# Turning the first expert tile's rows behind column tile 25 instead of 29 of the last attention block, in a graph attention and mixture-of-experts kernel

## The chip, the cores and the metric

The kernel runs on one core of a Trainium2 chip. A core has five engines that each work through a queue of their own: TensorE (PE, matmuls; its weight loads are listed as PEld), VectorE (DVE), ScalarE (ACT), GpSimd (POOL) and SyncE (SP, which here only issues DMAs). They wait for each other by semaphores. Matmul results go to PSUM, all other tiles lie in SBUF, and 16 DMA engines move data between these and HBM.

The metric is the time of one execution on the device in microseconds, as the median of several runs.

## The reference

One layer on 4096 tokens of width 256: a graph attention with four heads of 64 over a dense 4096 x 4096 adjacency, then a mixture of eight experts of which each token takes two. Both have a residual and a layer norm ahead.

```python
h = jnp.einsum('nd,hdk->hnk', x, W)
s_col = jnp.einsum('hnk,hk->hn', h, a1)
s_row = jnp.einsum('hnk,hk->hn', h, a2)
e = jax.nn.leaky_relu(s_row[:, :, None] + s_col[:, None, :], negative_slope=0.2)
e = jnp.where(adj[None, :, :] > 0, e, NEG_INF)
att = jax.nn.softmax(e, axis=-1)
h_prime = jnp.einsum('hij,hjk->hik', att, h)
out = jnp.transpose(h_prime, (1, 0, 2)).reshape(N, OUT_DIM)
y = jax.nn.elu(out) + x @ Wr + br
attention = gamma * (y - mean(y)) / sqrt(var(y) + LN_EPS) + beta
...
top_w, top_i = jax.lax.top_k(xf @ Wg + bg, 2)
top_w = jax.nn.softmax(top_w, axis=-1)
for e in range(8):
    h = jax.nn.gelu(xf @ W1[e] + b1[e], approximate=False)   # 256 -> 1024
    out = out + w_dense[:, e:e + 1] * (h @ W2[e] + b2[e])    # 1024 -> 256
```

## The kernel before

**Attention.** The 4096 rows are worked through in four blocks `a` of 1024 rows, and in each block the 4096 columns in 32 column tiles `j` of 128. A column tile has three steps. ScalarE turns the tile of the adjacency into a mask `am` (L1606). VectorE makes the unnormalised weights `w` of the four heads, one instruction of 128 x 1024 per head (L1689); ten buffers for `w` let it run up to two and a half tiles ahead of TensorE. TensorE then adds the weighted rows of each head into `acc` (L1198) and the sums of the weights into `den` (L1207). A matmul of `acc` fills 32 columns of the array and one of `den` two, and both are placed in different column groups, so that several run side by side. All of TensorE's instructions here hang on one hand-written chain: `queue` gives each an order behind the one queued last, and `order_of` does this for the small products in between, as long as `strict` is set.

**Between the tiles.** When a block is done, `finish_blocks(a)` works off what is left for its rows (normalising, elu, residual, both layer norms, the router's choice) in small steps: it is a generator, and one step is taken behind each column tile of the following block. Its last step is taken about tile 25; it works out each row's places in the experts' lists and issues 16 indirect DMAs on GpSimd (L1385), which scatter the rows, with their weights and ids, into `lists` in HBM. In this text, that is the scatter.

**The first expert tile.** In the last block, `a + 1 == NR`, the start of the expert stage is prepared within the attention. Behind tile 3, `plan_early` chooses the first expert tiles from what the lists hold so far, and `first_tile` asks for the first one's 256 rows, `xr0` (`load_rows_of`, issued at L571), and its first weights, `w10` (L600). Behind tile 29, `turn_first` turns those rows: `turn_rows_of` makes four transposes of 128 x 128 on TensorE (L607) into two PSUM banks `pt`, and copies each bank to `xT0` (L609). With `strict` set both copies are ScalarE's. Then `gelu_next` runs one activation on one column of `xT0` (L1589), whose only use is that the gelu table is loaded into ScalarE ahead of the first real gelu.

**After the last tile.** ScalarE and VectorE read `acc` and `den` (L1513, L1516, L1519). The pools of the attention are closed, and the expert stage's own tiles take their memory, so its loads can be issued only then. The loop over the expert tiles has two products each: `up` (L1872, with a gelu at L1876) and `down` (L1906). The rest of the last 1024 rows (`last_block`) goes in between them.

Of the kernel before, what the change touches and what calls it, by code (L numbers as in the profile page):

```python
# [44 lines left out]
def gat_then_moe(  # L45
# [23 lines left out]
    NT = N // P  # L69
# [6 lines left out]
    NR = N // R  # L76
# [142 lines left out]
    def forward(apart, stack):  # L219
# [39 lines left out]
        def turn_biases():  # L259
            pb = bank([P, E * FC], "pb")  # L260
            order_of(nc.tensor.transpose(pb, b1r, ident[: E * FC, : E * FC]))
            nc.vector.tensor_copy(bT, pb.rearrange("p (e f) -> p f e", e=E))
# [340 lines left out]
        def turn_rows_of(xr, xT):  # L603
            for c in range(DC):
                pt = bank([P, TT], "pt")
                for k in range(TT // CH):
                    order_of(nc.tensor.transpose(pt[:, ts(k, CH)], xr[:, k, ts(c, P)], ident))  # L607
                if c % 2 == 0 or strict[0] or (ordered[0] and given_out):
                    nc.scalar.copy(xT[:, c, :], pt)  # L609
                else:  # L610
                    nc.vector.tensor_copy(xT[:, c, :], pt)
# [3 lines left out]
        with ExitStack() as layer:  # L615
# [89 lines left out]
            def bounds_checked():  # L705

                nc.vector.tensor_reduce(strayed, limit, AX.X, OP.max)
                nc.vector.tensor_scalar(strayed, strayed, 0.5 * SPREAD, None, op0=OP.is_gt)
# [106 lines left out]
            def in_trace_order(start):  # L815

                before = {}
                for ins in nc.cur_bb.bb.instructions[start:]:
                    if ins.engine in before:
                        tc.add_manual_dep(  # L820
                            ins, before[ins.engine],
                            mybir.DependencyInfo(
                                mybir.DependencyClass.NoSync, mybir.DependencyReason.DATA
                            ),
                            reason="the order of the opening",
                        )
                    before[ins.engine] = ins.name
# [205 lines left out]
            def norm_steps(b):  # L1033

                with tc.issue_after(marks["top"]):
                    found = measured(b, fetched.pop(b))
                yield
                for t in range(TB):
                    normal_row(found, t)
                yield  # L1040
                pt = banks_turned()
                for t in range(TB):
                    turn_row(pt, found[0], t)
                keep_turned(b, pt)
                if b + 1 < NB:
                    fetched[b + 1] = rows_loaded(b + 1)
# [28 lines left out]
            def numbers_made():  # L1075

                if not apart:
                    nc.vector.tensor_scalar(brm, brm, -1.0, None, op0=OP.add)
                made_of_numbers()
# [132 lines left out]
            def attend(w, j, halves, sums_first=None):  # L1212


                def first_heads():
                    for half in halves:
                        for h in (1, 0):
                            rows_of_head(w, j, half, h)

                def other_heads():  # L1220
                    for half in halves:
                        for h in (1, 0):
                            weights_of_head(w, j, half, h)
                        rows_of_head(w, j, half, 2)
                    for half in halves:
                        rows_of_head(w, j, half, 3)
                        for h in (3, 2):
                            weights_of_head(w, j, half, h)

                parts = (first_heads, other_heads)  # L1230
                if sums_first is None:
                    sums_first = j in (0, NT - 1)
                for add in reversed(parts) if sums_first else parts:
                    add()
# [350 lines left out]
            def turn_first():  # L1585
                turn_rows_of(xr0, xT0)

            def gelu_next(known):
                nc.scalar.activation(warm, known, AF.Gelu)  # L1589
# [89 lines left out]
            else:  # L1679

                with tc.tile_pool(name="sep", bufs=2) as work:

                    def weigh(er, am, j, halves):
                        these = slice(halves[0], halves[-1] + 1)
                        mask = am.rearrange("p (s r) -> p s r", s=HB)
                        w = [[None] * H for half in range(HB)]
                        for h in ORDER:
                            wh = work.tile([P, HB, B], F32, tag="w", name="w", bufs=10)
                            marks["w"] = nc.vector.scalar_tensor_tensor(  # L1689
                                wh[:, these], er[:, these, h], eb[:, j, h : h + 1], mask[:, these],  # L1690
                                op0=OP.max, op1=OP.min,
                            ).ins
                            for half in range(HB):
                                w[half][h] = wh[:, half]
                        return w

                    both = list(range(HB))
                    ers = [er0, er1]
                    er = er0
                    pending = None  # L1700
                    norms, steps_of = {}, {}
                    ordered[0] = strict[0] = True
                    opened = len(nc.cur_bb.bb.instructions)
                    row = first_phase(weigh, norms)
                    in_trace_order(opened)
                    ordered[0] = False
                    with tc.issue_after(marks["w"]):
                        numbers_made()
                        bounds_checked()

                    def prepare_at(s):

                        for b in range(2, NB):
                            first = TB * b
                            if first - 3 <= s < first:
                                if b not in norms:
                                    norms[b] = norm_steps(b)
                                next(norms[b], None)
                            if first <= s < first + 4:
                                if s == first:  # L1720
                                    steps_of[b] = project_steps(b, True)
                                next(steps_of[b], None)

                    for j in range(TB):
                        prepare_at(TB + j)
                        attend(weigh(er, first_masks[:, j], j, [1]), j, [1])
                        if j == 0:
                            sums_turned(row)
                    for a in range(NR):
                        later = None  # L1730
                        for j in range(0 if a else TB, NT):
                            attend(
                                weigh(er, load_mask(a, j), j, both), j, both,
                                False if (a, j) == (NR - 1, NT - 1) else None,
                            )
                            if a == 0:
                                prepare_at(TB + j)
                            if pending:
                                next(pending, None)
                            if a == 1 and j == 1:  # L1740
                                turn_biases()
                            if a + 1 == NR and j == 3:
                                with tc.issue_after(marks["w"]):
                                    plan_early()
                                first_tile()
                            if a + 1 == NR and j == 29:
                                turn_first()
                                gelu_next(xT0[:, DC - 1, :1])
                            if j == 20 and a + 1 < NR:
                                later = ers[(a + 1) % 2]  # L1750
                                load_rows(later, (a + 1) * HB, HB, nc.scalar)
                        if a == 0:
                            mean_of_h()
                        er = later
                        if a + 1 < NR:
                            pending = finish_blocks(a)
                            next(pending)
                    strict[0] = False
# [350 lines left out]
```

## Time and profile before

| what | us |
|---|---|
| median of three runs | 1261.13 |
| lowest and highest of them | 1259.64, 1261.76 |
| the profiled execution's own time | 1260.56 |
| its span, first instruction to last | 1258.8 |
| last attention block ends, first expert matmul starts | 781.88 |
| PE, DVE, ACT, POOL busy | 1241.7, 845.5, 448.3, 240.4 |

The span is what the profile's shares refer to; all times in the text count from its start. A line of a timeline gives the start, the length, the engine, the line of the kernel, the operation, the tiles out<-in with their sizes, how many instructions are merged, and in brackets the engine's idle time before it with what ended that. "issue" means that the profile shows no wait, "remote" that a semaphore rose without an instruction that the profile could name. The start of a matmul is recorded, its end is modelled. A line of the table of stretches gives the stretch, its length, and then the busy time of PE, PEld, DVE, ACT and POOL with the number of their instructions, the clock granted to TensorE and the share of the DMA engines in use.

### The profile page before, as it was taken

To read this page: it belongs to the slowest core of one execution; us is meant where nothing else is said; L and a number is where in the kernel's file an instruction comes from. 1 tells how busy PE (TensorE), PEld (TensorE's weight loads), DVE (VectorE), ACT (ScalarE), POOL (GpSimd) and SP (SyncE) were. 2 spreads that over 40 slices of the span, in tenths; PEclk is the share of its full clock that TensorE was granted. 3 is DMA by queue.
4 is the path that set the end of the run, shared out by engine and by line. 5 is a ranking of instruction groups with operands and counts; after the bars stand their busy time and mean duration, and the time that the engine had idled before them with its cause. 6 is when DMAs were issued, how large, how long until landed. Compare 5 with 4: busy or idle time off the path is not lost.

```text
span 1258.8 us, 22720 instructions
## 1 busy us (share of the span) xinstructions
PE 1241.7 (99%) x8872; PEld 650.4 (52%) x8872; DVE 845.5 (67%) x1566; ACT 448.3 (36%) x918; POOL 240.4 (19%) x217
## 2 busy tenths in 40 slices
PE   9999999999999999999999999999999999999997
PEld 5444444332233332333325324888888876666686
DVE  7998887879999999999999995855111111111120
ACT  4332322265522365322655221533332332222322
POOL 4000000001002601006110024125322222122222
PEclk9999999999999999999999999999999999999999
DMA  6334433536533646334375422868998895455662
GB/s 215 118 118 126 155 107 102 166 104 145 177 114 103 225 112 201 116 94 158 107 178 183 133 70 77 276 171 219 259 236 239 227 219 116 102 139 105 140 160 37
DMA packets 155541, 190.23 MB, mean 151 GB/s; under 512 B 72312, under 2 KB 125680, under 8 KB 155040
## 3 DMA queue, kind: packets, MB, share of 16 engines
q1 hardware_dynamic: 133392, 145.39, 39.7%
q0 software_dynamic: 20544, 36.74, 13.2%
q10 hardware_dynamic: 1488, 6.55, 1.4%
q8 instruction: 71, 1.16, 0.4%
q14 instruction: 46, 0.38, 0.1%
HBM read 155.77 MB, written 29.74 MB: 147 GB/s over the span
## 4 chain that ended last, share of the span: by engine, by line
PE 93%; DVE 3%; issue 1%; ACT 1%; DMA 1%; POOLq 0%; SPq 0%; DVEq 0%; ACTq 0%
PE acc L1198 33%; PE po L1906 18%; PE ph L1872 17%; PE den L1207 17%; PE pr L1053 2%; DVE w L1689 2%; PE ph L1101 2%; PE ptx L1253 0%; DMA early<-lists 0%; PE acc L894 0%; PE pt L780 0%; PE ptr L1491 0%; PE po L1945 0%; PE pl L1264 0%; PE po L875 0%
## 5 line engine op out<-in xcount | busy, mean ns | idle before, releaser
L1198 PE MATMUL acc<-w,ha 128*32 128x512 f32 x4096 | 672.1, 593 | 2.3 <-ACT u L1401 0.9
L1689 DVE SCALAR_TENSOR_TENSOR w<-er,eb,am 128x1024 f32<-128x1024 f32 x496 | 605.9, 1275 | 36.2 <-PE den L1207 30.3
L1207 PE MATMUL den<-w,unit 128*2 128x512 f32 x2048 | 469.2, 592 | 0.4 <-issue 0.3
L1198 PEld LDWEIGHTS acc<-w,ha 128*32 128x32 f32 x4096 | 186.7, 110 | 293.7 <-issue 254.3
L1606 ACT ACTIVATE am<-adj 128x1024 bf16<-128x1024 int32 x124 | 130.6, 1054 | 347.8 <-DVE w L1689 213.1
L1872 PE MATMUL ph<-xT,w 128*128 128x256 f32 (+5 forms) x864 | 230.2, 424 | 2.1 <-issue 1.9
L1906 PE MATMUL po<-w,hT 128*128 128x256 f32 (+1 forms) x1040 | 229.7, 379 | 0.0
L1876 ACT ACTIVATE hT<-ph,bias 128x256 f32<-128x256 f32 (+5 forms) x216 | 111.1, 517 | 290.2 <-issue 185.8
L1906 PEld LDWEIGHTS po<-w,hT 128*128 128x128 f32 (+1 forms) x1040 | 195.7, 189 | 31.2 <-issue 3.1
L1919 DVE SCALAR_TENSOR_TENSOR o<-po,share,b2s 128x256 f32<-128x256 f32 (+2 forms) x66 | 31.7, 482 | 250.2 <-PE po L1906 211.4
L1872 PEld LDWEIGHTS ph<-xT,w 128*128 128x128 f32 x864 | 163.4, 190 | 62.0 <-issue 40.3
L1207 PEld LDWEIGHTS den<-w,unit 128*2 128x2 f32 x2048 | 94.7, 85 | 148.5 <-issue 140.0
L1931 POOL DMA_INDIRECT out<-o,ids x66 | 102.0, 1546 | 321.9 <-DMA out<-o,ids 136.4
L1385 POOL DMA_INDIRECT lists<-xe,at x64 | 88.3, 1379 | 267.6 <-issue 184.7
L1856 DVE STREAM_TRANSPOSE xT<-xr 128x512 f32<-128x512 f32 (+5 forms) x21 | 17.8, 850 | 34.0 <-PE ph L1872 31.2
L1053 PE MATMUL pr<-wr,xT 128*128 128x256 f32 x128 | 30.4, 381 | 0.2 <-ACT er L1147 0.2
L1894 ACT ACTIVATE b2s<-b2b,share 128x256 f32<-128x256 f32 x68 | 30.1, 499 | 0.0
L1121 POOL DMA_DIRECT2D residual<-rb x6 | 4.7, 784 | 121.2 <-DVE rb L1068 121.2
L1441 POOL DMA_DIRECT2D xf<-in_x x6 | 8.1, 1351 | 102.2 <-ACT xf L1440 102.2
L1053 PEld LDWEIGHTS pr<-wr,xT 128*128 128x128 f32 x128 | 24.1, 190 | 5.4 <-issue 0.9
L1101 PE MATMUL ph<-wall,xT 128*128 128x264 f32 x96 | 24.6, 399 | 0.0
L207 ACT ACTIVATE m<-y,off 128x256 f32<-128x256 f32 x48 | 23.7, 495 | 1.1 <-DVE off L215 0.6
(394 smaller groups left out, 618.8 us busy)
## 6 DMA issues: line engine op xcount, KB each, us to landing
adj<-in_adj SPq DMA_DIRECT2D x126, 512.0 KB
w<-in_L_ffn_W SPq DMA_DIRECT2D x54, 1024.0 KB
er<-parts ACTq DMA_DIRECT2D x3, 2048.0 KB
lists<-zeros POOLq DMA_DIRECT2D x8, 520.0 KB
residual<-rb POOLq DMA_DIRECT2D x8, 512.0 KB
rb<-residual SPq DMA_DIRECT2D x8, 512.0 KB
out<-y POOLq DMA_DIRECT2D x8, 512.0 KB
xb<-in_x SPq DMA_DIRECT2D x7, 512.0 KB
```

Of the source, the lines that this page charges most:

```text
L1053: order_of(nc.tensor.matmul(pr[:, k, :], turned[b][:, c, ts(t0 + k, P)], wr[:, c, :], start=(c == 0), stop=(c == DC - 1),))
L1101: order_of(nc.tensor.matmul(phs[t - t0], xT[:, c, ts(t, P)], wall[:, c, :], start=(c == 0), stop=(c == DC - 1),))
L1198: queue(nc.tensor.matmul(acc[half][h // 2][here : here + Q, :], ha[:, j, h * K + g * Q : h * K + (g + 1) * Q], w[half][h], start=(j == 0), ...
L1207: queue(nc.tensor.matmul(den[here : here + HB, :], unit[:, j, h, 1 - half : 1 - half + HB], w[half][h], start=(j == 0 and half == 0), stop ...
L1385: ins = nc.gpsimd.indirect_dma_start(lists, bass.IndirectOffsetOnAxis(ap=at[:, k, t : t + 1], axis=0), xe[:, t, :], None,).ins
L1606: nc.scalar.activation(am, at, AF.Relu, scale=2.0)
L1689: marks["w"] = nc.vector.scalar_tensor_tensor(wh[:, these], er[:, these, h], eb[:, j, h : h + 1], mask[:, these], op0=OP.max, op1=OP.min,).ins
L1872: order_of(nc.tensor.matmul(ph, job["w1"][:, c, ts(f, P)], xT[:, c, :], start=(c == 0), stop=(c == DC - 1),))
L1876: job["gelu"] = nc.scalar.activation(hT[:, f, :], ph, AF.Gelu, bias=job["bias"][:, f : f + 1]).ins
L1906: order_of(nc.tensor.matmul(po[:size], hT[:, f, k * CH : k * CH + size], w2[:, f, :], start=(f == 0), stop=(f == FC - 1),))
L1919: given_out.append(nc.vector.scalar_tensor_tensor(o[:size], po[:size], share[:size, k : k + 1], b2s[k][:size], op0=OP.mult, op1=OP.add,).ins)
L1931: added.append(add().ins)
```

## The change

`turn_first` is called behind column tile 25 of the last block, four tiles earlier. `gelu_next` stands alone behind the last column tile, 31, two tiles later than before. Nothing else is edited: the same instructions are issued, on the same engines and with the same buffers.

```diff
                                 with tc.issue_after(marks["w"]):
                                     plan_early()
                                 first_tile()
-                            if a + 1 == NR and j == 29:
+                            if a + 1 == NR and j == 25:
                                 turn_first()
+                            if a + 1 == NR and j == NT - 1:
                                 gelu_next(xT0[:, DC - 1, :1])
                             if j == 20 and a + 1 < NR:
                                 later = ers[(a + 1) % 2]
```

The two functions that it calls, and the one below them:

```python
def turn_first():
    turn_rows_of(xr0, xT0)

def gelu_next(known):
    nc.scalar.activation(warm, known, AF.Gelu)

def turn_rows_of(xr, xT):
    for c in range(DC):
        pt = bank([P, TT], "pt")
        for k in range(TT // CH):
            order_of(nc.tensor.transpose(pt[:, ts(k, CH)], xr[:, k, ts(c, P)], ident))
        if c % 2 == 0 or strict[0] or (ordered[0] and given_out):
            nc.scalar.copy(xT[:, c, :], pt)
        else:
            nc.vector.tensor_copy(xT[:, c, :], pt)
```

## The prediction

> **What bounds the kernel now.** I read the page first, then the chain of waits around the end of the last attention block, then the timeline of each engine there, then the times of single column tiles.
>
> ```profile
> span 1258.8 us, 22720 instructions
> ...
> PE 1241.7 (99%) x8872; PEld 650.4 (52%) x8872; DVE 845.5 (67%) x1566; ACT 448.3 (36%) x918; POOL 240.4 (19%) x217
> ...
> PE 93%; DVE 3%; issue 1%; ACT 1%; DMA 1%; POOLq 0%; SPq 0%; DVEq 0%; ACTq 0%
> ```
>
> TensorE carries 93% of the chain, so a microsecond of TensorE in the attention block or after it is a microsecond of the kernel, and an edit on ScalarE counts only if TensorE ends up waiting for it. But busy TensorE isn't TensorE at its rate, so I looked at the timeline of TensorE where the turn stands:
>
> ```profile
> 755.68 1.90 PE L1198 MATMUL acc<-w,ha 128*32 128x512 f32 x16
> ...
> 760.83 1.90 PE L1198 MATMUL acc<-w,ha 128*32 128x512 f32 x16
> ...
> 766.45 1.02 PE L1207 MATMUL den<-w,unit 128*2 128x512 f32 x2 [0.28 <-issue]
> 767.40 0.83 PE L607 MATMUL pt<-ident,xr 128*128 128x128 f32 x4
> 768.15 2.49 PE L1198 MATMUL acc<-w,ha 128*32 128x512 f32 x6
> 771.47 1.46 PE L1198 MATMUL acc<-w,ha 128*32 128x512 f32 x7 [0.82 <-issue]
> ```
>
> A column tile begins with the sixteen acc matmuls. Tiles 28 and 29 begin 5.15 us apart (755.68, 760.83), as nearly all do. Then tile 29 lasts to 768.15 with the turn (L607) at its end: 7.32 us. Tile 30's sixteen matmuls, 1.90 us elsewhere, come as six, an idle gap, seven and three more. The stretches of TensorE from tile start to tile start show the loss:
>
> ```profile
> 755.68:760.83 5.15, 5.15 (x52) 1.51 (x48) 4.89 (x5) 0.00 (x0) 4.23 (x4) 1.00 0.27 96
> 760.83:768.15 7.32, 7.04 (x56) 2.06 (x48) 3.46 (x3) 0.00 (x0) 5.49 (x7) 1.00 0.29 99
> 768.15:776.08 7.93, 6.98 (x47) 2.85 (x50) 2.57 (x2) 2.13 (x4) 1.91 (x2) 1.00 0.14 50
> 592.52:597.69 5.17, 5.17 (x54) 1.62 (x50) 5.17 (x5) 1.06 (x1) 4.33 (x3) 1.00 0.46 130
> ```
>
> The columns are length, busy time of PE, PEld, DVE, ACT and POOL with counts, granted clock and DMA share. The clock is 1.00 throughout, and the last line is a tile under the same scatter of rows (POOL L1385) one block earlier: no loss. Who waits meanwhile, on VectorE, ScalarE and GpSimd:
>
> ```profile
> 769.37 1.28 DVE L1689 SCALAR_TENSOR_TENSOR w<-er,eb,am 128x1024 f32<-128x1024 f32 x1 [5.09 <-PE pt L607]
> 771.49 1.28 DVE L1689 SCALAR_TENSOR_TENSOR w<-er,eb,am 128x1024 f32<-128x1024 f32 x1 [0.83 <-remote]
> ```
> ```profile
> 751.95 1.06 ACT L1606 ACTIVATE am<-adj 128x1024 bf16<-128x1024 int32 x1 [3.72 <-DVE w L1689]
> 772.37 0.65 ACT L609 COPY xT<-pt 128x256 f32<-128x256 f32 x2 [19.37 <-remote]
> 773.04 1.28 ACT L1589 ACT_TABLE_LOAD   x1
> ...
> 777.69 0.69 ACT L1513 ACTIVATE u<-acc,hbar 128x512 f32<-128x512 f32 x1 [3.16 <-PE acc L1198]
> ```
> ```profile
> 745.49 1.29 POOL L1385 DMA_INDIRECT lists<-xe,at  x1 [81.93 <-DVE at L1345]
> ...
> 769.39 0.97 POOL L1385 DMA_INDIRECT lists<-xe,at  x1 [0.30 <-issue]
> ```
>
> The transposes are recorded at 767.40 to 768.23, yet their copies on ScalarE start at 772.37, and the w that waits for tile 29's den (issued at 763.84) starts at 769.37. TensorE's word that it is done comes 4 to 5 us late, TensorE itself creeps, and all of it ends as the scatter (sixteen indirect DMAs, 745.49 to 769.39) ends.
>
> [...] Identity at 777.69 follows the gelu load without another.
>
> **The change part by part.**
>
> 1. The turn, moved from behind tile 29 to behind tile 25. It is four transposes of 0.27 to 0.33 us on TensorE and two copies of 0.38 us on ScalarE; it issues no DMA and passes no work of SP's or POOL's queue (the rows were asked for at 632.0 and must only have landed). Its price on TensorE: eight transposes (ptx, L1253) stretch a tile from 5.15 to 6.32 us (701.15 to 707.47), so 0.146 us each, 0.58 for four. It is paid before and after: 0.
>
> 2. The stall around it. Tile 29: 7.32 - 5.15 - 0.58 = 1.59 us. Tile 30: 7.93 - 5.15 = 2.78 us. Together 4.37 us. Is it the turn's, or the scatter's? The first sign of slowness on TensorE is the last den of tile 29 (a pair elsewhere, one by one here, 765.14 to 766.88), right at the turn; and the scatters of the two blocks before (399 to 433, 572 to 601) cost no column tile anything. Bounds: nothing gained if the scatter stalls whatever stands there, all 4.37 if it takes both. Behind tile 25 TensorE is at 745.38, just ahead of the first indirect DMA. I take 4.37 gained.
>
> 3. ScalarE's queue. The copies now come at about 746.2, between the masks am at 741.45 and 747.16. At worst they stand ahead of the earlier of these and hold it until 747, 5.5 us later than now; its first reader is the w at 751.78, so some 4 us of cover are left. Cost 0. Uncovered it would be 5.5 us of VectorE, which has ten w buffers (2.5 tiles, 12.9 us) of lead besides.
>
> 4. The w behind it. TensorE gives its 0.58 us at tile 25, so VectorE's buffers come free that much later: covered by the same lead. If the stall goes, the last two w (needed in tile 31) start at about 765 and 766 instead of 769.37 and 771.49.
>
> 5. The gelu table, moved to behind tile 31. One load of 1.28 us and one activation of 0.20 us. ScalarE has nothing from 753.0 (end of the last mask) to the first accumulator read at 777.69, apart from the copies. The load waits for no matmul of tile 31, only for the copies, so it may run right behind the mask. If it came behind the reads instead, ScalarE is idle from 779.24 to 782.00 and covers 1.48 us. The first gelu (783.80) waits for VectorE's bias. Cost 0; with cover gone 1.48 us.
>
> 6. What is late next. When attention ends 4.37 us sooner, the first expert tile needs xT0 and w10 (both asked for by 633.1). All other loads (SP from 782.16) are issued when the attention's memory is free and move along; the last scatter's landing at about 771.7 is still earlier than the end of attention at about 777.5. So the gain goes through to the end.
>
> Sum: 0 - 4.37 + 0. The profiled execution took 1260.56 us (span 1258.8 and 1.76 around it) and should take 1256.2, span 1254.4. The median of the runs is 0.57 above the profiled one: 1261.13 - 4.37 = 1256.8 us.
>
> **The rivals.**
>
> A, no change: the scatter's tail stalls TensorE and its semaphores whatever it is doing. For it: the den at 763.84 is already answered late, before the turn is reached; ten indirect DMAs follow at 1.27 us each there, faster than in the blocks before (mostly 2.3). Against it: the two clean scatters. Time 1261.1, within 1259.7 to 1262.0.
>
> B, part of it: only the part behind the turn (tile 30's 2.78) goes and the rest stays as the scatter's. 1258.3. It belongs to the faster cases.
>
> C, slower: transposes under a running scatter are what stalls TensorE, and behind tile 25 all sixteen indirect DMAs are still to come instead of two or three. The stall then happens at about 746, at the same price of 4.4 us, and what the scatter's end does to tile 29 stays: 1261.1 + 4.4 = 1265.5. It decides from the point where the new stall exceeds what leaves tile 29 and 30 by 2.5 us. For it: ptx transposes were never under a scatter in attention. Against it: at 745.38 the first indirect DMA isn't yet issued, and the turn takes under 1 us.
>
> **How the numbers follow.** Forecast with B: 0.57 (B 0.12 of it). A: 0.27. C: 0.16. About 0.2%, 2.5 us, is what a measurement of this kernel can tell from no change. The likeliest case alone runs from 1255.6 (4.37 and all of the 0.58, plus the spread of runs) to 1258.6. With A the range reaches to 1262.0, leaving C out: 1255.6 to 1262.0. Faster 0.57, same 0.27, slower 0.16.
>
> **What would show it.** In the new trace: L607 at about 745.4, its copies within 1 us of it, tile 25 with the turn at 5.75 us, tiles 29 and 30 at 5.15 each, the w no longer idle for 5 us, first expert matmul at about 777.5 instead of 781.88. A is right if tiles 29 and 30 still lose over 3 us without the turn; C if tile 25 or 26 loses over 2 us. I am wrong on ScalarE if a mask runs late and VectorE waits for it, or if the gelu load is found between the last matmul and the first gelu.

## The result, and the profile after

In 22 runs of each kernel, the changed one took 1258.28 us (1254.23 to 1263.21) and the kernel before 1261.57 (1259.33 to 1269.50). The chip of this comparison has no number on record and is called the first here. The ratio is 0.997, with a 95% interval of 0.9959 to 0.9981: 3.3 us shorter, between 2.4 and 5.2. The profiled execution took 1258.36 us, 2.2 less than that of before. The forecast was 1256.8 in a range of 1255.6 to 1262.0.

The page after, with the same three lines as before:

```profile
span 1256.7 us, 22720 instructions
...
PE 1239.8 (99%) x8872; PEld 647.8 (52%) x8872; DVE 845.1 (67%) x1566; ACT 448.2 (36%) x918; POOL 241.3 (19%) x217
...
PE 93%; DVE 3%; issue 1%; ACT 1%; DMA 1%; another core or an unknown queue 0%; POOLq 0%; SPq 0%; DVEq 0%; ACTq 0%
```

TensorE's busy time fell by 1.9 us: part of its stall was listed as busy. The stretches after, for tile 25 with the turn and for tiles 29 and 30:

```profile
740.24:746.11 5.87, 5.87 (x56) 1.82 (x53) 5.80 (x10) 1.06 (x1) 0.59 (x1) 1.00 0.09 38
761.58:766.73 5.15, 5.15 (x52) 1.51 (x48) 4.88 (x5) 0.00 (x0) 4.24 (x4) 1.00 0.24 82
766.73:771.88 5.15, 5.15 (x52) 1.51 (x48) 0.97 (x1) 0.00 (x0) 3.52 (x4) 1.00 0.26 91
```

Tiles 29 and 30 take 10.30 us instead of 15.25, and tile 25 pays 0.72 us for the turn. Who waited, on ScalarE and VectorE, after:

```profile
747.19 1.06 ACT L1606 ACTIVATE am<-adj 128x1024 bf16<-128x1024 int32 x1 [4.66 <-DVE w L1689]
748.15 0.63 ACT L609 COPY xT<-pt 128x256 f32<-128x256 f32 x2
748.80 1.28 ACT L1589 ACT_TABLE_LOAD   x1
...
752.29 1.06 ACT L1606 ACTIVATE am<-adj 128x1024 bf16<-128x1024 int32 x1 [1.99 <-DVE w L1689]
772.99 0.69 ACT L1513 ACTIVATE u<-acc,hbar 128x512 f32<-128x512 f32 x1 [19.65 <-PE acc L1198]
```
```profile
760.07 4.88 DVE L1689 SCALAR_TENSOR_TENSOR w<-er,eb,am 128x1024 f32<-128x1024 f32 x4 [0.27 <-PE den L1207]
765.22 2.48 DVE L1689 SCALAR_TENSOR_TENSOR w<-er,eb,am 128x1024 f32<-128x1024 f32 x2 [0.27 <-PE den L1207]
```

The 5.09 us of VectorE before its second last `w` are 0.27 now. The copies of the turn stand behind a mask and wait for nothing further, and the gelu table's load has slipped in ahead of the last mask, which it doesn't delay: that mask still waits 1.99 us for VectorE. The first expert matmul (L1873, one line lower than before) starts at 777.15 instead of 781.88, 4.73 us sooner. Yet the span shrank by only 2.1. The rest is lost a hundred microseconds later, beside the second scatter of the last rows (L1385, 868.92 to 878.84); TensorE's and ScalarE's timelines after:

```profile
871.74 5.34 PE L1873 MATMUL ph<-xT,w 128*128 128x256 f32 x24
877.40 1.13 PE L1873 MATMUL ph<-xT,w 128*128 128x256 f32 x4 [0.32 <-issue]
880.98 2.08 PE L1873 MATMUL ph<-xT,w 128*128 128x256 f32 x4 [2.45 <-ACT hT L1877]
```
```profile
876.87 0.47 ACT L1877 ACTIVATE hT<-ph,bias 128x256 f32<-128x256 f32 x1 [1.87 <-PE ph L1873]
880.46 1.20 ACT L1877 ACTIVATE hT<-ph,bias 128x256 f32<-128x256 f32 x3 [3.11 <-remote]
```

The product `up` has 32 matmuls; 28 are out by 878.5, ScalarE's gelus of them are released only at 880.46, and TensorE waits 2.45 us for these. Then the stretches show a thing that was not there before, a granted clock of 0.57:

```profile
880.00:884.00 4.00, 3.02 (x7) 2.48 (x8) 0.00 (x0) 2.11 (x6) 1.07 (x2) 0.57 0.48 109
```

The clock's record has half speed from 880.5 to 883.9. Compared instruction by instruction in TensorE's order, the changed kernel is 4.69 us ahead of the kernel before at 870 us, and 2.11 us ahead from 890 us to the end.

### The profile page after: what moved, and what is told of

The parts are those of the page before. It is cut to its first block, busy times and chain, and to the rows that moved or that the text cites. A ratio compares the mean times of both kernels' runs of the same rounds, so it can differ in the third digit from the quotient of the medians.

```text
span 1256.7 us, 22720 instructions
## 1 busy us (share of the span) xinstructions
PE 1239.8 (99%) x8872; PEld 647.8 (52%) x8872; DVE 845.1 (67%) x1566; ACT 448.2 (36%) x918; POOL 241.3 (19%) x217
## 2 busy tenths in 40 slices
DMA packets 155541, 190.23 MB, mean 151 GB/s; under 512 B 72312, under 2 KB 125680, under 8 KB 155040
## 4 chain that ended last, share of the span: by engine, by line
PE 93%; DVE 3%; issue 1%; ACT 1%; DMA 1%; another core or an unknown queue 0%; POOLq 0%; SPq 0%; DVEq 0%; ACTq 0%
PE acc L1198 33%; PE po L1907 18%; PE ph L1873 17%; PE den L1207 17%; PE pr L1053 2%; DVE w L1689 2%; PE ph L1101 2%; PE ptx L1253 0%; DMA early<-lists 0%; PE acc L894 0%; PE pt L780 0%; PE ptr L1491 0%; PE po L1946 0%; PE pl L1264 0%; PE po L875 0%
## 5 line engine op out<-in xcount | busy, mean ns | idle before, releaser
L1873 PE MATMUL ph<-xT,w 128*128 128x256 f32 (+5 forms) x864 | 231.4, 425 | 2.9 <-ACT hT L1877 2.6
L1873 PEld LDWEIGHTS ph<-xT,w 128*128 128x128 f32 x864 | 163.8, 191 | 63.4 <-issue 38.7
L1385 POOL DMA_INDIRECT lists<-xe,at x64 | 89.0, 1391 | 268.0 <-issue 184.8
```

Of the source, the lines that this page charges most:

```text
L1385: ins = nc.gpsimd.indirect_dma_start(lists, bass.IndirectOffsetOnAxis(ap=at[:, k, t : t + 1], axis=0), xe[:, t, :], None,).ins
L1873: order_of(nc.tensor.matmul(ph, job["w1"][:, c, ts(f, P)], xT[:, c, :], start=(c == 0), stop=(c == DC - 1),))
```

## The experiments

The theories, as the expectations name them: T, the turn standing behind tile 29, beside the late part of the scatter, is what stalls. S, the scatter's end stalls TensorE whatever stands there. R, chance of one execution. G, the gelu table's load, not the turn. P, any shift of the rhythm by 0.7 us ends the stall. Later ones are told in the expectation itself.

Rows with the same chip number share one set of runs of the kernel before. Over the seven comparisons, that kernel falls into two groups, and this turned out to be the key. "Late" counts the instructions that raise TensorE's semaphore and behind whose start the trace records no update of it for over 2 us. It is an upper bound: the traces lack some updates (995 to 1013 are recorded of some 1033 where the count isn't 0, and 1033 to 1036 where it is), and a missing one counts as late even where its reader went on in time. Paired one to one with the recorded updates, 7 to 11 are over 2 us late in each of those six profiles.

| chip | before, us | run | this, us | ratio, 95% interval | tiles 29, 30 | late |
|---|---|---|---|---|---|---|
| first | 1261.57 | the change | 1258.28 | 0.9970, 0.9959 to 0.9981 | 5.15, 5.15 | 11 (before 23) |
| 10 | 1253.82 | e1 before | 1253.79 | 0.9999, 0.9991 to 1.0008 | 5.85, 5.17 | 0 |
| 10 | | e2 gelu only | 1255.00 | 1.0004, 0.9996 to 1.0012 | 5.85, 5.17 | 0 |
| 10 | | e3 turn and gelu at 25 | 1253.59 | 0.9993, 0.9985 to 1.0002 | 5.15, 5.15 | 0 |
| 10 | | e4 turn twice | 1254.44 | 1.0005, 0.9997 to 1.0013 | 5.86, 5.17 | 0 |
| 4 | 1253.87 | e5 the change | 1253.87 | 1.0000, 0.9991 to 1.0008 | 5.15, 5.15 | 0 |
| 4 | | e6 turn twice | 1254.39 | 1.0003, 0.9994 to 1.0011 | 5.85, 5.17 | 0 |
| 7 | 1261.69 | e7 turn at 12 | 1256.34 | 0.9956, 0.9942 to 0.9971 | 5.15, 5.14 | 24 |
| 7 | | e8 scatter doubled | 1286.33 | 1.0174, 1.0147 to 1.0201 | 8.44, 28.01 | 15 |
| 9 | 1261.46 | e9 gelu only | 1261.21 | 0.9993, 0.9984 to 1.0002 | 7.28, 7.91 | 12 |
| 9 | | e10 scatter later | 1264.70 | 1.0030, 1.0016 to 1.0043 | 5.85, 5.18 | 12 |
| 3 | 1253.72 | e11 scatter spaced | 1256.60 | 1.0020, 1.0012 to 1.0028 | 5.86, 5.17 | 0 |
| 11 | 1253.80 | e12 the same | 1256.41 | 1.0017, 1.0004 to 1.0030 | 5.85, 5.17 | 0 |

**On a chip where nothing stalls.** e1 is the kernel before, unedited.

> The kernel before, unchanged, a second profile of it. If the stall belongs to the place of the turn (theory T), tile 29 and tile 30 together lose 3 to 5 us again and the first expert matmul starts at about 782. If the stall was a chance of that one execution (theory R), it is gone or stands in other tiles. Time ratio 1.000 in both.

e2 moves the gelu table alone, e3 moves the turn with the table behind it, e4 turns the rows twice:

```diff
 e2   if a + 1 == NR and j == 29:
          turn_first()
+     if a + 1 == NR and j == NT - 1:
          gelu_next(xT0[:, DC - 1, :1])
 e3
-     if a + 1 == NR and j == 29:
+     if a + 1 == NR and j == 25:
          turn_first()
          gelu_next(xT0[:, DC - 1, :1])
 e4
-     if a + 1 == NR and j == 29:
+     if a + 1 == NR and j in (25, 29):
          turn_first()
+     if a + 1 == NR and j == NT - 1:
          gelu_next(xT0[:, DC - 1, :1])
```

> The turn stays behind tile 29, only the gelu load goes behind tile 31. Theory T and the theory that the end of the scatter alone makes the stall (S): the load has no part in it, time as before, 1261.6 within 1.5, tiles 29 and 30 lose 3 to 5 us. If the gelu load were the cause (G): 1258.3, and the two tiles are clean.

> The turn and the gelu load both behind tile 25. T: like the changed kernel, 1258.3 within 1.5, tiles 29 and 30 at 5.15 us each. G: 1261.6. Nothing waits for the load in either place.

> The turn is made behind tile 25 and once more behind tile 29 (the second writes the same values again), the gelu load behind 31. T: the stall is back, tiles 29 and 30 lose 3 to 5 us beyond 0.6 for each turn, time about 1262.2. If the place of the first turn counts only because it moves the tiles by 0.6 us or gives VectorE and the scatter another rhythm (theory P): tiles 29 and 30 lose at most the second turn's 0.6 us, time about 1258.9.

The kernel before takes 1253.8 us on this chip, 7.7 less than on the first, and its tile 29 shows why. The stretch of tile 29 and the turn's copies in e1:

```profile
760.88:766.73 5.85, 5.85 (x56) 1.80 (x48) 5.59 (x5) 0.09 (x1) 4.87 (x4) 1.00 0.24 81
```
```profile
766.64 0.65 ACT L609 COPY xT<-pt 128x256 f32<-128x256 f32 x2 [13.57 <-PE pt L607]
```

The same program, the same turn under the same scatter (745.6 to 771.8), costs 0.70 us, and its copies start as the transposes end, not 4 us later. So the program alone doesn't make the stall. All four runs lie within 0.07% of the kernel before. T, S, G and P can't be told apart here; a stall in every execution, whatever the chip, is excluded.

**The change once more, on another such chip.**

> The changed kernel once more, timed against the kernel before on one chip. If the stall behind tile 29 is what the change takes away, the gain goes with the kernel before: where that is again near 1261 us, T (the turn's place) and S (the scatter's end alone) both let this run be 3 to 4 us shorter with tiles 29 and 30 at 5.15 us each; where that is near 1254 us, as on the last chip, there is no stall to take away and the two are within 1 us. R (chance of one execution): no difference on any chip, and a difference only in a profile.

> The rows turned behind tile 25 and once more behind tile 29, the gelu table behind the last tile. Where the kernel before is near 1261 us: T (a turn behind tile 29, beside the scatter's end, is what stalls): tile 29 and 30 stall again by about 4.4 us, the time is that of the kernel before plus up to 0.7 us for the second turn. G (the table load or its order, not the turn): no stall, 0.7 us over the changed kernel. P (anything that shifts the last tiles by 0.7 us breaks the rhythm): no stall either. Where the kernel before is near 1254 us: 0.6 to 0.7 us over the changed kernel, no stall.

The ratio of the change is 1.0000, and the second turn of e6 shows as 0.70 us in tile 29 (0.5 us between the medians of e6 and e5, within their noise). The expectation's second branch held in both: where there is no stall, the change is worth nothing. TensorE in e5, at the place where the changed kernel lost time on the first chip:

```profile
871.72 7.07 PE L1873 MATMUL ph<-xT,w 128*128 128x256 f32 x32
```

All 32 matmuls go through in 7.07 us, with the DMA engines as full as on the first chip (a share of 1.12 from 876 to 880, there 1.10), so a lack of DMA bandwidth isn't what holds TensorE up there.

**On a chip that stalls: the turn's place, and the scatter's length.** e7 moves the turn far ahead of the scatter; e8 leaves it and doubles the scatter, each copy going into a list that nobody reads. (`...` stands for lines left out.)

```diff
 e7
-     if a + 1 == NR and j == 29:
+     if a + 1 == NR and j == 12:
          turn_first()
+     if a + 1 == NR and j == NT - 1:
          gelu_next(xT0[:, DC - 1, :1])
 e8   behind each indirect DMA to lists, for b == 2 * HB
+     ins = nc.gpsimd.indirect_dma_start(
+         spare, bass.IndirectOffsetOnAxis(ap=at[:, k, t : t + 1], axis=0),
+         xe[:, t, :], None,
+     ).ins
+     ...
```

> The rows turned behind tile 12 of the last attention block, 14 tiles before any scatter; the gelu table behind the last tile. T (a turn beside the scatter's end is what stalls) and S (the scatter's end alone): tile 12 at 5.85 us, tiles 29 and 30 as S or T have them, so where the kernel before is near 1261 us T gives 1257 to 1258 us and S stays at 1261 us. Where the kernel before is near 1254 us nothing stalls behind the scatter and the turn costs its 0.7 us wherever it stands: within 0.8 us of the kernel before.

> The kernel before with each of the 16 indirect DMAs of the third pair's scatter followed by a copy of itself into a spare list, so 32 of them from 745 us on; the turn stays behind tile 29. D (the number of indirect DMAs by itself delays TensorE's semaphores): tile 29 and 30 stall by 2 us or more on any chip, and waits of 4 to 7 us for TensorE show up. K (the delay is a property of the chip of the first comparison): where the kernel before is near 1254 us, tile 29 stays at 5.85 us and tiles 30 and 31 at 5.15 us, no update of TensorE's semaphores comes over 2 us late, and what the total grows by (0 to 10 us) falls behind the attention, where the second half of the copies ends at about 790 us and the expert loads wait for the queue.

Tiles 29 and 30 of e7:

```profile
761.10:766.25 5.15, 5.15 (x53) 1.51 (x49) 4.88 (x5) 0.00 (x0) 4.23 (x4) 1.00 0.25 88
766.25:771.39 5.14, 5.14 (x52) 1.50 (x48) 0.97 (x1) 0.00 (x0) 3.92 (x5) 1.00 0.26 91
```

The time, 1256.34, is a little under the 1257 to 1258 that T expected. S falls: the scatter's last four DMAs (767.2 to 772.0) run beside tile 30 and the start of tile 31, and nothing stalls. P gets no support either: until 763 us VectorE, GpSimd and TensorE follow each other in e7 as in the kernel before, all 0.2 to 0.3 us later. The `den` issued at 763.84 there is answered after 5.51 us, the same `den` here, issued at 764.10, after 0.61. Two things differ from then on: what comes next in TensorE's queue, and the pace of GpSimd, whose next indirect DMA comes 1.27 us behind that of 763.03 in the kernel before and 2.32 us behind that of 763.30 here. Only the first was edited; which of the late update and the faster pace brings the other, these profiles don't tell. (On chips 7 and 9 the kernel before was timed but not profiled; e9 below, with the turn in place, shows the stall on chip 9.)

e8 has the turn at its old place, with 32 indirect DMAs from 746.88 to 792.92. Its stretches for tiles 29 and 30, and the copies of the turn:

```profile
762.22:770.66 8.44, 7.09 (x56) 2.10 (x49) 3.45 (x3) 0.00 (x0) 6.43 (x7) 1.00 0.29 103
770.66:798.67 28.01, 17.35 (x46) 3.19 (x49) 2.57 (x2) 2.23 (x4) 17.25 (x17) 0.86 0.24 86
```
```profile
787.74 0.37 ACT L609 COPY xT<-pt 128x256 f32<-128x256 f32 x1 [33.34 <-remote]
790.55 0.37 ACT L609 COPY xT<-pt 128x256 f32<-128x256 f32 x1 [2.44 <-remote]
```

The transposes start at 769.2 to 769.5 and their copies 18 and 21 us later. Tile 30 takes 28 us and runs freely again from 796 us, 3 us behind the last DMA. So the stall lasted nearly as long as the scatter. D was expected "on any chip" and was tried on one that stalls, so this run doesn't part D from K; beside the first profile, whose scatter ends at 770.4 and whose copies start at 772.4, it shows that the scatter sets the length.

**On another chip that stalls: the gelu table, and the scatter later.** e9 is e2 again. e10 makes the scatter's list positions `at` later: four steps of the generator later, and behind a mark in VectorE's work on the weights:

```diff
+ for _ in range(4 * (b == 2 * HB)):
+     yield
+ placed = nc.vector.tensor_copy(at, pos).ins
+ if b == 2 * HB and "w" in marks:
+     after(placed, marks["w"], "the lists behind the masked rows")
- nc.vector.tensor_copy(at, pos)
```

> The turn stays behind tile 29, the gelu table alone goes behind the last tile. Where the kernel before is near 1261 us: T (the turn beside the running scatter) expects no gain, 1260.5 to 1262 us, tile 29 over 7 us and tile 30 near 7.9 us; G (the table load, not the turn) expects the whole gain, 1256 to 1258.5 us, tile 29 at 5.85 us. Where the kernel before is near 1254 us both expect no difference, and the run says nothing.

> The turn stays behind tile 29; the third pair's list positions are made some 11 rows of the weights later, so that the scatter starts about 12 us later (near 757 us instead of 745) and ends near 782 us. Where the kernel before is near 1261 us: T (a turn stalls while the scatter still has several indirect DMAs to go, until its last) expects the stall behind tile 29 to last on to the scatter's end: tiles 29 and 30 together 10 to 20 us longer than 11 us, and a time of 1268 us or more. E (only a turn in the last 10 us of the scatter stalls, since there the indirect DMAs follow each other at 1.27 us) expects the turn, now 8 us behind the scatter's start, to cost its 0.7 us and no stall in tiles 29 and 30, with 1257 to 1262 us. Where the kernel before is near 1254 us: no stall, within 2 us of the kernel before.

Tiles 29 and 30 of e9, and tiles 29, 30 and 31 of e10:

```profile
762.36:769.64 7.28, 7.02 (x56) 2.01 (x49) 3.45 (x3) 0.00 (x0) 5.45 (x7) 1.00 0.29 101
769.64:777.55 7.91, 7.28 (x48) 2.62 (x50) 2.60 (x2) 2.13 (x4) 1.94 (x2) 1.00 0.14 51
```
```profile
762.47:768.32 5.85, 5.85 (x56) 1.80 (x49) 5.57 (x5) 0.11 (x1) 4.85 (x4) 1.00 0.23 78
768.32:773.50 5.18, 5.18 (x50) 1.54 (x53) 0.27 (x1) 2.12 (x4) 3.88 (x4) 1.00 0.29 104
773.50:788.68 15.18, 11.70 (x52) 2.10 (x45) 1.45 (x2) 1.27 (x2) 6.78 (x7) 0.89 0.20 70
```

e9: with the table moved and the turn left, the stall is there to within 0.04 us (7.32 and 7.93 in the first profile). G falls, and R with it: two profiles from two comparisons, one size, and a median that repeats.

e10: the scatter now runs from 760.37 to 782.25. The turn, 7.4 us behind its start, costs 0.70 us and tile 30 is clean, so T in the form it had there (a turn stalls while the scatter still has several DMAs to go) falls. E was right on tiles 29 and 30, but not on the time: tile 31, with no turn near it, takes 15.18 us up to the first expert matmul, where the changed kernel has 5.27, and here too TensorE is free some 2 us behind the scatter's last DMA (matmuls follow each other again from 784.4). The turn is therefore not the only thing that a scatter can hold up. What both places share is that TensorE's even stream of `acc` and `den` is about to end (at the turn; at the close of the attention). The first late update belongs to an instruction issued 18.4 us behind the scatter's start in the kernel before (763.84) and 14.1 us in e10 (774.44).

**Spaced scatters.** Is it the density of the indirect DMAs? In e11 and e12 (one kernel) GpSimd does two small additions behind each pair of them, in every scatter, and the next pair is ordered behind them:

```diff
+ ...
+ for _ in range(2):
+     with tc.issue_after(ins):
+         ins = nc.gpsimd.tensor_tensor(gap, xe[:, t, :32], xe[:, t, 32:64], OP.add).ins
+ spaced.append(ins)
```

> The turn stays behind tile 29; in every scatter GpSimd does two small additions behind each pair of indirect DMAs (about 0.7 us a pair), so that no more than two of them follow each other at 1.27 us. Where the kernel before is near 1261 us: Q (what holds TensorE's semaphore updates back is the dense run of indirect DMAs, and the turn only meets it) expects tile 29 at 5.85 us and tile 30 at 5.15 us, no update over 2 us late also in the scatters between 850 and 890 us, and 1254 to 1257 us. T (the turn beside a running scatter, dense or not) expects the stall behind tile 29 to stay and to last 2 to 4 us longer, as the scatter does: 1261 to 1266 us. Where the kernel before is near 1254 us: no stall, 0 to 4 us over the kernel before for the longer scatters.

> The spaced scatters once more, in the hope of a chip on which the kernel before stalls. Where the kernel before is near 1261 us: Q (the dense run of indirect DMAs holds TensorE's semaphore updates back) expects tiles 29 and 30 at 5.85 and 5.15 us, no update over 2 us late anywhere, and, with the 2.9 us that the spacing cost on a chip without the stall, 1256 to 1258 us. T (the turn beside a running scatter, dense or not) expects the stall behind tile 29 to last on to the scatter's end near 778 us, 8 us or more in tiles 29 to 31, and 1264 us or more. Where the kernel before is near 1254 us: 1256 to 1258 us, no stall, and Q and T stay undecided.

Both fell on chips without the stall, so Q stays undecided. The other profiles speak for it, without showing it. The stalls of the kernel before, e8, e9 and e10 stand in runs of 7 to 13 indirect DMAs that are 1.27 to 1.28 us apart, where e7 and the changed kernel, on chips that stall, have at most four in a row there. In e10 the run comes first: VectorE's last `w` ends at 768.6, the DMAs are 1.27 us apart from 768.54 on, and the first late update is that of 774.44. But e1 and e5 have the same dense second scatter without a late update, so density alone isn't enough. What e11 and e12 show is the price, 2.6 to 2.9 us: the last DMA comes at 776.84 in e11 where e1 has it at 770.79, and TensorE is 3.0 us behind e1 by 798 us, with a spell at half clock from 788.4 to 791.8.

**What stays open.** Why TensorE's semaphores come late in some comparisons and not in others: each numbered chip was used once, so the chip isn't parted from the time at which it was used. Whether the second turn (e4, e6), the direct test of P, brings the stall back where one exists: both fell on chips without it. Whether a looser scatter would end the stall; and whether tile 31 of e10 stalls by the same mechanism as tile 29 or only looks alike.

## Why the prediction was right, and where not

**The place of the stall and its owner** (step 2). Right, and shown where the stall exists: without the turn there it is gone (the change, e7), and moving the table alone leaves it (e9). That the turn's place decides is shown; how it does so is not. Of the two bounds, nothing and 4.37 us, the upper one was the right choice there. Tiles 29 and 30 gave 4.95 us, tile 31 another 0.53 (5.80 to 5.27), tile 25 took 0.72 and started 0.03 later: in all 4.73 at the first expert matmul; forecast 4.37.

**What the prediction couldn't see.** It took one profile's stall for the kernel's. On four chips it isn't there, and where the change was timed on such a chip (e5), rival A's difference, none, is what comes out, by another mechanism than A's. That the forecast was measured on a chip that stalls was luck. A itself (the scatter's tail, whatever stands there) falls with e7. The fact used against A, that the scatters of earlier blocks cost no tile anything, holds, but it proves less than it seemed: no turn stands in them, and their DMAs are mostly 2.3 us apart.

**The late word.** In the profile before, 4 us lie between the recorded end of the transposes (768.23) and their copies (772.37). In e1 the same copies start at 766.64, within 0.2 us of the recorded end, so the usual course has no such 4 us in it: they belong to the stall.

**The turn's own price** (step 1). Forecast 0.58 and cancelling; measured 0.70 behind tile 29, 0.72 behind tile 25 and 0.93 behind tile 12 (e7), so nearly cancelling: right in the sum, 0.12 to 0.14 short in the term.

**ScalarE's queue and the gelu table** (steps 3 and 5). Cost 0 in both, right: e9 and e2 differ from the kernel before by less than 0.1%. The order was not as told: the copies stand behind the mask of 747.19, not ahead of it, and the load lies ahead of the last mask, not behind. The cover named for it, an idle ScalarE, was there in either case.

**VectorE's lead** (step 4). Right: its last two `w` start at 765.22, forecast 765 and 766.

**The gain goes through to the end** (step 6). This is the step that failed in part. The attention ended at 777.15, forecast 777.5, but the lead of 4.69 us at 870 us is 2.11 from 890 us on. Step 6 asked which loads would be late next and found none, rightly. It didn't ask where else the same late semaphores occur. Beside the second scatter of the last rows, TensorE already lost 2.16 us in the kernel before (the first profile against e1, which does not lose there), and loses 4.74 in the changed one (against e5), with 2.45 us of idle time and a spell at half clock in it. In e7 it loses 2.18, without that spell. So the term put at nothing, the later cost of coming sooner, measured 2.58 us in this profile, and part of that is how the clock's spell happened to fall (see the last section). The median's gain, 3.3 us, lies between the profile's 2.1 and the forecast.

**Rival C.** Its mechanism is real in the large (e8: a turn in a scatter that goes on stalls to its end), but its place was wrong: behind tile 25 the scatter is only beginning (745.52, as the turn starts), and in e10 a turn 7.4 us into one passes freely.

## What to carry to other kernels

A stall in one profile may belong to the chip: profile the kernel before again elsewhere before its stall is priced as a gain, and time a change on more than one chip. Where such a stall shows, try moving odd TensorE work (transposes with their own semaphore waits) away from the late part of a long GpSimd scatter; here that cost nothing where no stall occurs and gained 3 to 5 us where one does. And when a stall is taken away, look for the other places with the same signature, since the work that comes sooner meets them in another phase.

## What was not expected of the hardware

**Late updates of TensorE's semaphores, on some chips only.** In the six profiles of chips where the kernel before needs 1261 to 1262 us, 11 to 24 instructions see no update for over 2 us (7 to 11 in a pairing one to one), by this count up to 10 us (the copies in e8 waited 18 and 21), most of them beside GpSimd's indirect DMAs; in the eight of chips where it needs 1254 us, none does. The program and its DMA traffic are the same for the kernel before on both kinds of chip (155541 packets and 190.23 MB in the first profile and in e1), and the clock doesn't part them (0.993 to 0.999 there, 0.996 to 0.999 here). The wait that TensorE's sequencer holds ahead of the turn shows it from another side. Line L607 in the kernel before, first chip, and in e1:

```profile
L607 PEldq EVENT_SEMAPHORE  x1: 51/51/51, 765.0 to 765.0; - x1
```
```profile
L607 PEldq EVENT_SEMAPHORE  x1: 51/51/51, 763.5 to 763.5; - x1
```

In e1 it passes 2.6 us behind the tile's start, in the kernel before 4.2 us, although the tile starts within 0.1 us of the same time and the semaphore that it waits for last rose at 736.3 and 736.4 us. So TensorE's own queue is held up too, not only the word it sends, and it is so by the first entry of the turn, before a transpose has run.

**The half clock.** The clock's record of the changed kernel has one spell at half speed beside this stall, 3.41 us long (880.51 to 883.93). It begins 2.0 us into an idle time of 2.45 and goes on for 2.9 us behind its end. The idle times of 1.90 us (before) and 1.73 us (e7) at the same place brought none, while one of 1.77 us there in e9 did, and so did 1.61 and 1.48 us in e11 and e12, elsewhere. So the length of an idle time alone doesn't decide. The kernel before, no spell, and e9, a spell:

```profile
884.53 1.13 PE L1872 MATMUL ph<-xT,w 128*128 128x256 f32 x4 [1.90 <-issue]
```
```profile
885.94 1.76 PE L1873 MATMUL ph<-xT,w 128*128 128x256 f32 x4 [1.77 <-issue]
```

In the changed kernel this spell and the next (880.51 and 1252.57) start 109 times 3.413 us apart. Counted in steps of that length from a spell of the same profile, and by an estimate from the recorded busy times, TensorE was busy for 33% of the stretch ahead of the spell in the changed kernel (877.10 to 880.51) and 48% in e9, and for 55% and 49% of the emptiest stretch there in the kernel before (880.76 to 884.18) and e7, which had none. This is no rule: a stretch of 48% near the end of the kernel before (1249.40 to 1252.82) brought none either. What decides is not shown. What can be carried off is that a stall of this size may be paid twice: here 2.45 us of idle time, and 3.41 us of half clock that began in it.

The 22 times of the changed kernel go with the mean clock, though which of the two leads is not shown: 1254.2 us at a mean of 0.999, 1255.7 to 1256.0 at 0.998, 1256.3 to 1259.2 at 0.997, 1259.8 to 1263.2 at 0.994 to 0.996.
